# Four edits to a four-layer kernel: one scratch tile, the place of some clearings, an early bias, and the order of the last half block

## The chip, the cores and the metric

The kernel runs on one core of a Trainium2 chip. The core has five engines with their own instruction queues: TensorE (PE in the profile, its weight loads PEld), VectorE (DVE), ScalarE (ACT), GpSimd (POOL) and SyncE (SP), which here issues DMAs. They run side by side and wait for each other through semaphores. The metric is the device time of one execution in microseconds. Before the change it is 1390.49 us, the median of three runs (1388.63 to 1393.59).

## The reference, cut to what matters

Four transformer layers, each an attention and a feed-forward part, on 8 x 512 tokens of 128 columns in float32. Every part normalizes its input and adds its output to the residual:

```python
x = x + _L0_attn_ref(_layernorm(x), ...)   # spiking linear attention
x = x + _L0_ffn_ref(_layernorm(x), ...)    # 16 experts, top 2, gelu
x = x + _L1_attn_ref(_layernorm(x), ...)   # linear attention, elu + 1
x = x + _L1_ffn_ref(_layernorm(x), ...)    # gated, with chosen rows through 8 experts
x = x + _L2_attn_ref(_layernorm(x), ...)   # softmax attention, 16 heads of 64
x = x + _L2_ffn_ref(_layernorm(x), ...)    # low-rank experts, top 2, gelu
x = x + _L3_attn_ref(_layernorm(x), ...)   # causal convolution of 21 taps
x = x + _L3_ffn_ref(_layernorm(x), ...)    # fp4 quantized silu(gate) * up, then down
```

In the last part both the input and `h = silu(gate) * up` are rounded to a 4-bit grid in blocks of 16: the block's largest magnitude over 6 is the scale, the quotients are rounded, and the result is multiplied by the scale again. In layer 2's attention the queries have a bias `q_b`, and the scores are divided by 8.

## The kernel before, in words

The tokens lie in eight blocks of 512, each held on chip as 128 partitions by 4 tiles by 128 columns (`x[b]`). The program is recorded in the order in which the code is written; each engine executes its own instructions in that order, and waits where an operand comes from another engine. Tiles come from pools. A pool's tag has a number of buffers that are handed out in turn, and when a pool is closed, the next one's tiles take its memory: the first instruction that writes there waits for the last ones that used the old tiles.

*Layer 0's feed-forward part* (`layer0`) runs 128 units, one for each block and expert. For each unit TensorE makes the hidden values, ScalarE the Gelu, TensorE the second product, VectorE multiplies by the gate into a tile `pr` (line 607, in `second_half`), and GpSimd adds `pr` to the block's sum (line 611). `pr` comes from the pool `f0`, which is closed after the layer.

*Layer 1* (`layer1`) first records some preparations: two columns of ones in the tiles `vts`, a row of ones in the three tiles `zts` (line 1274), a matrix `top_row` with a first row of ones (lines 1275 and 1276), two small loads `ebs`, a tile `nought` of zeros (line 1281), and 15 DMAs from SP that write `nought` to device memory (seven to `back`, line 1283, eight to `slots_in`, line 1288). Then a loop over eight iterations runs the list `stages`; a stage with lag k works on block i + k. Among them are `project_q` (TensorE, then on ScalarE a Relu, line 880, and an exponential, line 881), `project_kv`, the key map (VectorE, line 885), `gather` (keys by values on TensorE), `attend`, `finish` (layer 0's last product for the blocks 3 to 7), and norms: mean and variance on VectorE (lines 758 to 761), reciprocal root on GpSimd (lines 246 and 247), scaling on ScalarE (line 769). `f_scale` stores each block's normalized rows by SP to `by_rows`, from where GpSimd gathers the chosen rows after the loop (line 1066). After the loop comes a hand-written order for the chosen rows; its last instructions scatter rows to `back` (line 1233) and add to the residual on GpSimd (line 1052 and line 1378).

*Layers 2 and 3* (`late`) run in 64 frames, one for each block and pair of heads, with the steps of layer 2's experts and layer 3 hung into them. The first instruction scales the query bias on VectorE (`qb`, line 2652, with the weights' blob `a2` as input); `queries` then makes keys on VectorE (line 1560) and queries on ScalarE (line 1559, which reads `qb`), and `first_scores` multiplies them.

*The end* (`end`) works off the last two blocks of layer 3: L is block 6, and A and B are the halves of block 7 (two tiles each). For each of them `quant_x1` and `quant_x2` round the input, `turn_x` transposes it, `gated` makes gate and up products and a tanh on ScalarE, and `gated_v` the factors. With `at_end` and `thirds`, ScalarE also copies half of up to a tile `prod` (line 2161), VectorE makes `(tanh + 1) * gate` (line 2164), and GpSimd multiplies the two (line 2166); without `thirds` VectorE does the second product too (line 2168). `quant_h1` (`fp4_scale`, lines 1401 to 1406) finds the blocks' scales and quotients. `fp4_round` rounds (VectorE: mask, line 1418; scaling of the mask, line 1421; add and subtract, lines 1422 and 1423) and multiplies by the scale on GpSimd (line 1424). `turn_h` transposes (line 2216) and copies (line 2219), `down` makes the last product, adds it to the residual (line 2100) and stores the rows (line 2239). `keep_clock(n)` issues n matmuls of 128x128 whose results nobody reads. The order is that of the code:

```python
                L.down()
                keep_clock(6)
                B.turn_x()
                ...
                B.quant_h1(1)
                A.turn_h(0)
                B.quant_h2_tile(1, 0)
                B.quant_h2_tile(1, 1)
                A.down()
                keep_clock(22)
                B.turn_h(1)
                B.down()
```

Of the kernel before, what the change touches and what calls it, by code (L numbers as in the profile page):

```python
# [17 lines left out]
F32 = mybir.dt.float32  # L18
# [146 lines left out]
def body(ctx, tc, dram, spans, x_in, ib, it, ic, ei, out):  # L165
# [114 lines left out]
    acc = []  # L280
    last_acc = first.tile([P, NB - 3, TB], F32, tag="acc", name="acc")
# [5 lines left out]
    def layer0():  # L287
# [7 lines left out]
        with ExitStack() as st:  # L295
# [302 lines left out]
            def second_half(b, e, hm, gs):  # L598
                po = bank()
                for i in range(4):  # L600
                    mm(
                        po[32 * i : 32 * (i + 1), :],
                        w2[:, e, :, :].rearrange("p a o -> p (a o)"),
                        hm[:, i, :],
                    )
                pr = acc[b] if e == 0 else wp.tile([P, TB], F32, tag="pr", name="pr")
                nc.vector.scalar_tensor_tensor(  # L607
                    pr, po, f0["b2"][:, e : e + 1], gs, ALU.add, ALU.mult
                )
                if e > 0:  # L610
                    nc.gpsimd.tensor_tensor(acc[b], acc[b], pr, ALU.add)  # L611
# [245 lines left out]
    def layer1():  # L857
# [9 lines left out]
        with tc.tile_pool(name="l1", bufs=2) as wp, tc.tile_pool(name="l1c", bufs=1) as once:  # L867
# [398 lines left out]
            with tc.manual_schedule():  # L1266
# [6 lines left out]
                for zt in zts:  # L1273
                    nc.gpsimd.memset(zt[64:65, :], 1.0)
                nc.gpsimd.memset(top_row, 0.0)
                nc.gpsimd.memset(top_row[:1, :], 1.0)
# [3 lines left out]
                nought = wp.tile([P, J, D], F32, tag="zo", name="nought")  # L1280
                nc.gpsimd.memset(nought, 0.0)
                for b in range(1, NB):
                    nc.sync.dma_start(
                        back[b * TB : (b + 1) * TB, :].rearrange("(j p) d -> p j d", p=P), nought
                    )
                for b in range(2):
                    blank[b] = [
                        nc.sync.dma_start(
                            slots_in[b][k * TB : (k + 1) * TB, :].rearrange("(j p) d -> p j d", p=P),
                            nought,  # L1290
                        ).ins
                        for k in range(4)
                    ]
                for i in range(NB):
                    for f, lag in stages:
                        if 0 <= i + lag < NB and (f, i) != (turn_, 0):
                            f(i + lag)
# [135 lines left out]
    def late():  # L1433
# [11 lines left out]
        with tc.tile_pool(name="a2", bufs=2) as wp, tc.tile_pool(name="l3", bufs=1) as lp:  # L1445
            N = NB * 8
            qb = wp.tile([P, 8], F32, tag="qb", name="qb", bufs=1)
# [582 lines left out]
            def layer3(b, xp, tile_, part=(0, J), conv_bank="one", h_tag="h"):  # L2030
# [156 lines left out]
                def quant_h2_tile(i, j):  # L2187
                    sc, a = t["fh", i]
                    k = slice(22 * j, 22 * (j + 1))
                    h = tile_("h", h_tile)  # L2190
                    fp4_round(lp, h[:, 2 * i + j, :], sc[:, k], a[:, k, :], 22)
# [31 lines left out]
                def down():  # L2223
                    ht = tile_("ht", None)
                    po = bank()
                    for j in range(j0, j1):
                        for k, _ in thirds:
# [6 lines left out]
                            )  # L2234
                    added(po)
# [149 lines left out]
            def end():  # L2385
# [51 lines left out]
                L.down()  # L2437
                keep_clock(6)
                B.turn_x()
                B.gated(2, True)  # L2440
                B.gated(3, True)
# [209 lines left out]
            with tc.manual_schedule():  # L2651
                nc.vector.tensor_scalar(qb, a2["qb"], 0.125, None, ALU.mult)
# [93 lines left out]
```

## Time and profile before

| | us |
|---|---|
| median of three runs | 1390.49 |
| the profiled execution, its own time | 1387.75 |
| its span, first to last instruction | 1385.6 |
| PE busy | 1323.9 (96%) |
| DVE busy | 1024.1 (74%) |
| ACT busy | 1011.0 (73%) |
| POOL busy | 646.3 (47%) |
| mean granted TensorE clock | 0.997 of full speed |

The profile is of one execution, whose times count from its first instruction. A line of the timeline gives the start, the duration, the engine, the line of the kernel, the instruction, its output and inputs by the program's names, the shape, and how many instructions of one kind are merged; in brackets stand the idle time of that engine just before, and what ended it. Line numbers in the text are those of the kernel before.

Layer 0 ends and layer 1 begins at about 381 us of the span, layer 1 ends at about 499 us, and the end part begins at about 1326 us.

### The profile page before, as it was taken

To read this page: it belongs to the slowest core of one execution; us is meant where nothing else is said; L and a number is where in the kernel's file an instruction comes from. 1 tells how busy PE (TensorE), PEld (TensorE's weight loads), DVE (VectorE), ACT (ScalarE), POOL (GpSimd) and SP (SyncE) were. 2 spreads that over 40 slices of the span, in tenths; PEclk is the share of its full clock that TensorE was granted. 3 is DMA by queue.
4 is the path that set the end of the run, shared out by engine and by line. 5 is a ranking of instruction groups with operands and counts; after the bars stand their busy time and mean duration, and the time that the engine had idled before them with its cause. 6 is when DMAs were issued, how large, how long until landed. Compare 5 with 4: busy or idle time off the path is not lost.

```text
span 1385.6 us, 33142 instructions
## 1 busy us (share of the span) xinstructions
PE 1323.9 (96%) x12910; PEld 704.4 (51%) x12910; DVE 1024.1 (74%) x2173; ACT 1011.0 (73%) x2050; POOL 646.3 (47%) x758
## 2 busy tenths in 40 slices
PE   7889999999989899999999999999999999999997
PEld 3762222222277655547447455555555555555576
DVE  6786666677477778863783689788788897887876
ACT  6859999999977656655684686777767767667632
POOL 6756667765632533230472453453443634424432
PEclk9999999999999999999999999999999999999999
DMA  5015555555280111241201101102011010110000
GB/s 181 1 25 163 170 145 149 150 152 145 62 278 28 28 40 35 65 115 30 73 21 36 45 2 22 31 2 43 11 23 23 9 33 20 23 23 10 2 9 16
DMA packets 125309, 84.47 MB, mean 61 GB/s; under 512 B 61984, under 2 KB 103712, under 8 KB 124769
## 3 DMA queue, kind: packets, MB, share of 16 engines
q1 hardware_dynamic: 123423, 78.43, 20.3%
q0 software_dynamic: 1152, 2.36, 0.6%
q8 instruction: 102, 1.67, 0.5%
q10 hardware_dynamic: 578, 1.57, 0.3%
q14 instruction: 54, 0.44, 0.1%
HBM read 64.29 MB, written 22.23 MB: 62 GB/s over the span
## 4 chain that ended last, share of the span: by engine, by line
PE 37%; DVE 14%; ACT 10%; issue 2%; POOL 1%; DMA 0%; DVEq 0%; ACTq 0%; POOLq 0%
PE ps L250 27%; PE ps L1598 8%; ACT ex L1677 6%; DVE nm L1671 5%; ACT prod L2065 2%; DVE acc L2051 1%; PE ps L2248 1%; DVE fa L1422 1%; DVE fa L1406 1%; ACT q L1559 1%; DVE fsc L1401 1%; ACT xn L1481 1%; DVE fa L1423 1%; DVE fm L1418 1%; DVE k L1560 1%
## 5 line engine op out<-in xcount | busy, mean ns | idle before, releaser
L1677 ACT ACTIVATE ex<-ps,nm 128x512 f32<-128x512 f32 x512 | 345.2, 687 | 172.3 <-DVE nm L1671 172.2
L1671 DVE TENSOR_REDUCE nm<-ps 128x2 f32<-128x1024 f32 x256 | 300.9, 1210 | 39.1 <-PE ps L250 39.0
L250 PE MATMUL ps<-q,k 64*64 64x512 f32 (+1 forms) x2240 | 258.3, 564 | 8.9 <-ACT ex L1677 5.7
L250 PE MATMUL ps<-ex,vs 128*64 128x512 f32 x1024 | 233.8, 598 | 1.1 <-DVE sm L1691 1.1
L1692 POOL TENSOR_TENSOR vs<-v,sm 128x256 f32<-128x256 f32 x128 | 78.6, 614 | 292.9 <-DVE sm L1691 268.6
L1598 PE MATMUL ps<-xt,blob_a 64*64 64x512 f32 x912 | 207.8, 589 | 0.1
L611 POOL TENSOR_TENSOR acc<-acc,pr 128x512 f32<-128x512 f32 x120 | 165.9, 1382 | 87.2 <-DVE pr L607 78.8
L595 ACT ACTIVATE hm<-ps,blob_f 128x1536 f32<-128x1536 f32 x128 | 196.2, 1533 | 0.0
L607 DVE SCALAR_TENSOR_TENSOR pr<-ps,blob_f,gs 128x512 f32<-128x512 f32 x120 | 90.0, 750 | 87.2 <-PE ps L250 76.6
L250 PEld LDWEIGHTS ps<-q,k 64*64 64x64 f32 x2240 | 74.8, 132 | 152.0 <-ACT ex L1677 78.2
L250 PE MATMUL ps<-h,w 32*128 32x512 f32 x1024 | 148.3, 643 | 1.1 <-ACT hm L594 0.6
L250 PEld LDWEIGHTS ps<-ex,vs 128*64 128x64 f32 x1024 | 68.0, 136 | 152.9 <-issue 128.1
L250 PE MATMUL ps<-hm,w 128*32 128x512 f32 x1024 | 136.8, 606 | 5.1 <-DVE pr L607 2.7
L2066 POOL TENSOR_TENSOR acs<-acs,prod 128x512 f32<-128x512 f32 x96 | 124.0, 1292 | 23.9 <-ACT prod L2065 19.4
L1598 PE MATMUL ps<-blob_a,ct 64*64 64x128 f32 x1824 | 118.6, 269 | 0.0
L1598 PE MATMUL ps<-blob_a,xt 64*64 64x128 f32 x1824 | 118.5, 269 | 0.0
L1598 PEld LDWEIGHTS ps<-blob_a,ct 64*64 64x64 f32 x1824 | 106.2, 133 | 0.0
L1677 ACT ACTIVATION_READ_ACCUMULATOR ex<-ps,nm 128x1 f32 x512 | 105.0, 205 | 0.0
L1598 PEld LDWEIGHTS ps<-blob_a,xt 64*64 64x64 f32 x1824 | 103.0, 133 | 0.0
L250 PEld LDWEIGHTS ps<-h,w 32*128 32x128 f32 x1024 | 41.1, 183 | 108.7 <-ACT hm L594 103.4
L594 ACT ACTIVATE hm<-ps,blob_f 128x512 f32<-128x512 f32 x128 | 88.0, 687 | 8.5 <-PE ps L250 8.3
L1598 PEld LDWEIGHTS ps<-xt,blob_a 64*64 64x64 f32 x912 | 61.7, 133 | 31.9 <-issue 28.4
(366 smaller groups left out, 2212.3 us busy)
## 6 DMA issues: line engine op xcount, KB each, us to landing
gs<-gates SPq DMA_DIRECT2D x248, 128.0 KB, 3.0
gates<-plain SPq DMA_DIRECT2D x16, 256.0 KB, 3.2
ht<-turned_h SPq DMA_DIRECT2D x20, 180.0 KB, 2.8
turned_h<-hb SPq DMA_DIRECT2D x40, 88.0 KB, 2.3
blob_f<-in_f SPq DMA_DIRECT2D x1, 2560.0 KB, 9.2
blob_a<-in_a SPq DMA_DIRECT2D x1, 2056.0 KB
x<-in_x SPq DMA_DIRECT2D x8, 256.0 KB, 5.7
plain<-turned SPq DMA_DIRECT2D x32, 64.0 KB, 2.2
```

The lines of the kernel that those rows point to most:

```text
L250: nc.tensor.matmul(out_, lhs, rhs, start=start, stop=stop)
L594: nc.scalar.activation(hm[:, 0, :], p1, AF.Gelu, bias=bias)
L595: nc.scalar.activation(hm[:, 1:, :], p3, AF.Gelu, bias=bias)
L607: nc.vector.scalar_tensor_tensor(pr, po, f0["b2"][:, e : e + 1], gs, ALU.add, ALU.mult)
L611: nc.gpsimd.tensor_tensor(acc[b], acc[b], pr, ALU.add)
L1401: nc.vector.tensor_reduce(sc, s3, AX.X, ALU.max, apply_absolute_value=True)
L1598: ins = nc.tensor.matmul(*args, **kw).ins
L1671: nc.vector.tensor_reduce(nm, ps, AX.X, ALU.max, negate=True)
L1677: nc.scalar.activation(ex[kt][:, i, :], ps[:, i, :], AF.Exp, bias=nm[:, i : i + 1], accum_out=sm[:, kt, i : i + 1],)
L1692: nc.gpsimd.tensor_tensor(vs[:, tiles, :, :], vs_[n][:, tiles, :].rearrange("p j (i n) -> p j i n", i=2), sm[:, tiles, :].unsqueeze(3).to_ ...
L2065: nc.scalar.activation(p, src, AF.Copy, scale=w)
L2066: nc.gpsimd.tensor_tensor(t["acs"], t["acs"], p, ALU.add)
```

## The change

1. In `second_half` the product of the very last unit (block 7, expert 15) is written to a tile of the pool `norm` (tag `xt`), which stays open through the whole kernel, and not to one of `f0`.
2. The fills of `zts`, `top_row` and `nought`, and the 15 DMAs that write zeros, are recorded at the start of the third iteration of layer 1's loop, not ahead of the loop. `vts` and `ebs` stay.
3. `qb` lies in the pool `const`, and is scaled at the start of the fifth iteration of layer 1's loop.
4. In `end`, `gated` of the tiles 2 and 3 (half B) is called without `thirds`. `down` is split into products and output: L's products move behind B's `gated`, into another PSUM bank, and L's residual add and store behind `A.down()`. B's last rounding is done by a new `quant_h2_pair`: mask and its scaling for both tiles at once, add and subtract tile by tile, and the last product for the first tile on GpSimd and for the second on VectorE. The calls of `keep_clock` become 17 and 13, where they were 6, 8 and 22.

```diff
+                elif (b, e) == (NB - 1, 15):
+                    pr = norm.tile([P, TB], F32, tag="xt", name="pr")
...
                 for i in range(NB):
+                    if i == 2:
+                        cleared()
+                    if i == 4:
+                        nc.vector.tensor_scalar(qb, a2["qb"], 0.125, None, ALU.mult)
                     for f, lag in stages:
...
+                def quant_h2_pair(i):
                     sc, a = t["fh", i]
+                    m = lp.tile([P, 44, 16], F32, tag="fm44", name="fm")
+                    nc.vector.tensor_scalar(
+                        m.bitcast(I32), a.bitcast(I32), 0x7F800000, None, ALU.bitwise_and
+                    )
+                    nc.vector.tensor_scalar(m, m, 1.0, 1.5 * 2.0**22, ALU.max, ALU.mult)
+                    for j, engine in enumerate((nc.gpsimd, nc.vector)):
+                        k = slice(22 * j, 22 * (j + 1))
+                        nc.vector.tensor_tensor(a[:, k, :], a[:, k, :], m[:, k, :], ALU.add)
+                        nc.vector.tensor_tensor(a[:, k, :], a[:, k, :], m[:, k, :], ALU.subtract)
+                        engine.tensor_tensor(
+                            tile_("h", h_tile)[:, 2 * i + j, :].rearrange("p (n k) -> p n k", k=16),
+                            a[:, k, :],
+                            sc[:, k].unsqueeze(2).to_broadcast([P, 22, 16]),
+                            ALU.mult,
+                        )
...
                 B.quant_x2()
-                L.down()
-                keep_clock(6)
+                keep_clock(17)
                 B.turn_x()
-                B.gated(2, True)
-                B.gated(3, True)
+                B.gated(2, True, False)
+                B.gated(3, True, False)
                 A.quant_h1(0)
                 A.quant_h2(0)
                 B.gated_v(2)
                 B.gated_v(3)
-                keep_clock(8)
+                po = L.down_products(bank("c"))
                 B.quant_h1(1)
                 A.turn_h(0)
-                B.quant_h2_tile(1, 0)
-                B.quant_h2_tile(1, 1)
+                B.quant_h2_pair(1)
                 A.down()
-                keep_clock(22)
+                L.down_out(po)
+                keep_clock(13)
                 B.turn_h(1)
                 B.down()
...
             with tc.manual_schedule():
-                nc.vector.tensor_scalar(qb, a2["qb"], 0.125, None, ALU.mult)
                 xts[0] = t[0]["next"]
```

More of the change, by code (lines that the diff above doesn't have):

```diff
@@ L280, in body @@
     acc = []
+    qb = const.tile([P, 8], F32, tag="qb", name="qb")
     last_acc = first.tile([P, NB - 3, TB], F32, tag="acc", name="acc")
@@ L605, in second_half @@
                     )
-                pr = acc[b] if e == 0 else wp.tile([P, TB], F32, tag="pr", name="pr")
+                if e == 0:
+                    pr = acc[b]
+                elif (b, e) == (NB - 1, 15):
+                    pr = norm.tile([P, TB], F32, tag="xt", name="pr")
+                else:
+                    pr = wp.tile([P, TB], F32, tag="pr", name="pr")
                 nc.vector.scalar_tensor_tensor(
@@ L1272, in layer1 @@
                     nc.gpsimd.memset(v[:, :, P : P + 1], 1.0)
[L1273 to L1276, printed above, removed]
                 for k, name in enumerate(("eb1", "eb2")):
@@ L1279, in layer1, with cleared @@
                     nc.sync.dma_start(ebs[:, k, :], dram["rows"][:, lo:hi].partition_broadcast(P))
[L1280 to L1287, printed above, removed]
-                        nc.sync.dma_start(
[L1289 to L1293, printed above, removed]
+                def cleared():
+                    for zt in zts:
+                        nc.gpsimd.memset(zt[64:65, :], 1.0)
+                    nc.gpsimd.memset(top_row, 0.0)
+                    nc.gpsimd.memset(top_row[:1, :], 1.0)
+                    nought = wp.tile([P, J, D], F32, tag="zo", name="nought")
+                    nc.gpsimd.memset(nought, 0.0)
+                    for b in range(1, NB):
+                        nc.sync.dma_start(
+                            back[b * TB : (b + 1) * TB, :].rearrange("(j p) d -> p j d", p=P), nought
+                        )
+                    for b in range(2):
+                        blank[b] = [
+                            nc.sync.dma_start(
+                                slots_in[b][k * TB : (k + 1) * TB, :].rearrange("(j p) d -> p j d", p=P),
+                                nought,
+                            ).ins
+                            for k in range(4)
+                        ]
                 for i in range(NB):
+                    if i == 2:
+                        cleared()
+                    if i == 4:
+                        nc.vector.tensor_scalar(qb, a2["qb"], 0.125, None, ALU.mult)
                     for f, lag in stages:
@@ L1446, in late @@
             N = NB * 8
-            qb = wp.tile([P, 8], F32, tag="qb", name="qb", bufs=1)
             xts, vs_, qks, exs, outs, cts = {}, {}, {}, {}, {}, {}
@@ L2185, in quant_h2 @@
                     fp4_round(lp, pair(i), *t["fh", i], 44)
-                def quant_h2_tile(i, j):
+                def quant_h2_pair(i):
                     sc, a = t["fh", i]
-                    k = slice(22 * j, 22 * (j + 1))
-                    h = tile_("h", h_tile)
-                    fp4_round(lp, h[:, 2 * i + j, :], sc[:, k], a[:, k, :], 22)
+                    m = lp.tile([P, 44, 16], F32, tag="fm44", name="fm")
[12 more added lines that the diff above has]
+                            ALU.mult,
+                        )
                 def blocks_h(i):
@@ L2223, in down, with down_products @@
                 def down():
+                    down_out(down_products(bank()))
+                def down_products(po):
                     ht = tile_("ht", None)
-                    po = bank()
                     for j in range(j0, j1):
@@ L2234, in down, with down_out @@
                             )
+                    return po
+                def down_out(po):
                     added(po)
```

## The prediction

> **What bounds the kernel now.** The page first: one core, TensorE busy 96% at full clock, and a chain of waits that it can follow back only to 496 us.
>
> ```profile
> span 1385.6 us, 33142 instructions
> PE 37%; DVE 14%; ACT 10%; issue 2%; POOL 1%; DMA 0%; DVEq 0%; ACTq 0%; POOLq 0%
> ```
>
> So a share says little: the edits touch three short places, each with its own last wait. I read each in the timeline (start, duration, engine, line, and in brackets the idle time before it with its releaser). Place one is the hand-over from layer 0 to layer 1:
>
> ```profile
> 380.69 1.89 PE L250 MATMUL ps<-blob_l,xt 128*128 128x256 f32 x8
> 380.83 1.27 POOL L611 TENSOR_TENSOR acc<-acc,pr 128x512 f32<-128x512 f32 x1 [0.80 <-DVE pr L607]
> 382.13 0.60 ACT L880 ACTIVATE ex<-ps 128x512 f32<-128x512 f32 x1 [2.16 <-POOL acc L611]
> 383.29 0.58 ACT L880 ACTIVATE ex<-ps 128x512 f32<-128x512 f32 x1
> 384.86 0.23 POOL L246 TENSOR_SCALAR rs<-mv 128x4 f32<-128x4 f32 x1
> 386.53 1.65 ACT L769 ACTIVATE xn<-x,nb,rs 128x128 f32<-128x128 f32 x4 [1.03 <-POOL nb L763]
> ```
>
> ScalarE stands 2.16 us until GpSimd has added layer 0's last product. Place two is the start of layer 2:
>
> ```profile
> 498.38 1.28 POOL L1378 TENSOR_TENSOR x<-x,blob_bc 128x512 f32<-128x512 f32 x1
> 498.98 0.72 DVE L2652 TENSOR_SCALAR qb<-blob_a 128x8 f32<-128x8 f32 x1 [1.02 <-POOL x L1052]
> 499.61 0.74 DVE L1560 TENSOR_SCALAR k<-ps,blob_a 128x512 f32<-128x512 f32 x1
> 499.78 0.69 ACT L1559 ACTIVATE q<-ps,qb 128x512 f32<-128x512 f32 x1 [3.69 <-DVE qb L2652]
> 500.52 1.95 PE L250 MATMUL ps<-q,k 64*64 64x512 f32 x16 [1.86 <-ACT q L1559]
> ```
>
> An 8-column scaling stands ahead of the first keys and queries, and TensorE waits for both. Place three is the end, VectorE and GpSimd taking turns:
>
> ```profile
> 1362.72 0.69 DVE L2100 TENSOR_TENSOR x<-x,ps 128x512 f32<-128x512 f32 x1
> 1368.94 1.38 POOL L1424 TENSOR_TENSOR h<-fa,fsc 128x704 f32<-128x704 f32 x1 [4.07 <-DVE fa L1423]
> 1370.28 1.81 POOL L2166 TENSOR_TENSOR h<-s,prod 128x352 f32<-128x352 f32 x2
> 1372.12 0.89 DVE L1401 TENSOR_REDUCE fsc<-h 128x44 f32<-128x704 f32 x1 [2.47 <-POOL h L2166]
> 1376.90 0.81 DVE L1421 TENSOR_SCALAR fm<-fm 128x352 f32<-128x352 f32 x1
> 1378.91 0.79 POOL L1424 TENSOR_TENSOR h<-fa,fsc 128x352 f32<-128x352 f32 x1 [1.40 <-DVE fa L1423]
> 1382.03 0.42 DVE L2100 TENSOR_TENSOR x<-x,ps 128x256 f32<-128x256 f32 x1 [2.87 <-PE ps L250]
> ```
>
> VectorE idles 2.47 us for two GpSimd products queued behind a third; after the last quantization only transposes, copies and products remain.
>
> **The change, part by part.**
>
> *Last product in the norms' pool.* Layer 1's first Relu takes over layer 0's scratch memory, so it waits for the last reader of the `pr` buffers: the add that ends at 382.10. Now that reader is the add before (ended 380.02), and what ends last is the query projection on TensorE, ended 380.85. So the first Relu could start 1.25 us sooner. But the key Relu (383.29) reads a projection that TensorE ends at 380.69 + 1.89 = 382.58, so from there only 383.29 - 382.62 = 0.67 us is left. From the key Relu run, without slack, the exponential, the value copy, the key map (385.04) and TensorE's gather (385.83). I take 0.67; ends 0 and 1.25.
>
> *Clearings at the third iteration.* Out of GpSimd's queue go six fills, 382.35 to 384.78. They stood ahead of the reciprocal root at 384.86; ScalarE's 1.03 us idle goes, but its next Relu then waits for TensorE, so nothing is added to the 0.67. They come back where GpSimd idles 5.91 us (390.4 to 396.3): 2.4 us fit. Of the 15 zero-fill DMAs on SP the last was issued at 406.26, and the first store of normalized rows at 407.23. They now start about 7 us later but behind the same two weight loads (2,560 and 2,056 KB), which are what held them (one issue took 8.7 us). If that store slips, its reader is GpSimd's row gather at 462.42, over 50 us later. I count nothing; if both covers failed, the 2.4 us of fills would show.
>
> *Query bias early.* It comes to VectorE behind the fourth key map, at 409.3. Small scalings without company cost 0.17 to 0.18 us (line 1107, 128x18: 0.176); in this iteration VectorE takes up the gather's result without idling, so I charge 0.1, ends 0 and 0.72 (its row at 498.98). At the start of layer 2 the keys move up to 498.98, when VectorE's list of waits is done, and end at 499.72; ScalarE's queries no longer wait for `qb`, only for the same GpSimd add (ended 498.45) and scatter, and run beside the keys. TensorE starts at 499.78 instead of 500.52: 0.74. The old row ran to 499.70, when GpSimd's add at 498.38 ended. Would that add hold the keys too, the gain would be 0.1 at most. But all 64 key rows lie between 0.732 and 0.752 us, with GpSimd busy beside many, so I keep 0.74; ends 0 and 0.74.
>
> *The end.* (i) The residual add at 1362.72 moves behind the quantizations; the next reduction moves up by 0.61 (1362.72 to 1363.33), and all to the last rounding with it. (ii) The two GpSimd products (1.81) and two ScalarE copies are replaced by two VectorE instructions of 0.52. Four such instructions to the next reduction took 2.15 us at 1331.26 to 1333.41; so the reduction starts at 1368.71 - 0.61 + 2.15 = 1370.25, not 1372.12: 1.87 so far. GpSimd's 1.38 us product, which it must also await, ends at 1369.7. (iii) From that reduction to the mask took 2.53 us, unchanged. Mask and scaling run whole (1.12, from 1365.85 to 1366.97) and not twice by halves; then four half adds and subtracts and VectorE's own last product: 0.56 + 0.46 + 0.56 + 0.56 + 0.53 = 2.67. Ready at 1370.25 + 6.32 = 1376.57, where the old one was at 1379.70. (iv) GpSimd's half product (0.79) now runs amid VectorE instructions with two SBUF operands. These rows show what that costs:
>
> ```profile
> 112.11 1.28 POOL L611 TENSOR_TENSOR acc<-acc,pr 128x512 f32<-128x512 f32 x1
> 112.66 1.28 DVE L477 TENSOR_TENSOR one<-eq,place 128x512 f32<-128x512 f32 x1
> 731.48 1.29 POOL L2066 TENSOR_TENSOR acs<-acs,prod 128x512 f32<-128x512 f32 x1
> 732.71 0.63 POOL L1692 TENSOR_TENSOR vs<-v,sm 128x256 f32<-128x256 f32 x1
> 732.80 1.08 DVE L2097 TENSOR_TENSOR acc<-acc,acs 128x512 f32<-128x512 f32 x1 [0.43 <-POOL acs L2066]
> ```
>
> Alone this form takes 0.68 (median of line 462). Begun while GpSimd had 0.73 and 0.54 us to go, it lost 0.60 and 0.40: it stood until about 0.13 before GpSimd's end. Here GpSimd must first outlast one VectorE add, then holds back the next for its 0.79 less 0.13 at its end and, I estimate, 0.17 that pass before VectorE asks: about 0.49. Ready at 1377.06. [...] (v) The last tile's transposes wait for the residual add behind it (0.34 + 0.12): 1377.52, before 1379.75. From there the old end took 2.28 us, six products among them; three of these now run earlier, so 1.95. VectorE's last add starts at 1379.47, not 1382.03: 2.56. The moved products and the other filler matmuls lie on TensorE while it would idle: 12 products (2.94) end by 1370, when the transposes want it; 13 fillers of 0.23 end about 1375.5, before the first half is ready at 1376.3. Ends: 3.05 without the lock; 0.9 if the lock takes 1.5 (two of line 462's worst case, 1.43 - 0.68) and (i) gives nothing.
>
> Sum: 0.67 - 0.1 + 0.74 + 2.56 = 3.9 us. The profiled execution took 1387.75 with a span of 1385.6; it becomes 1383.9. It is below all three runs shown (median 1390.49), from which I take the same 3.9: 1386.6.
>
> **The rivals.**
> [...]
> - *The early gains are absorbed*, some later wait of layer 1 or 2 ending where it did: only the end counts, 2.5, 1388.0. For it: 100 us lie between place one and two. Against: each iteration of layer 1 is one ring, VectorE's kv at 403.18 to TensorE, back to VectorE at 407.13, to the key map at 408.63 and TensorE's gather, about 8.1 us a turn, and no landing is in it.
> - *The end is given back*: the moved 256 KB store now goes out about 1.5 us before the last, whose landing is the end. Stores of that size land in 2.3 us, of the last one's in 1.8; fully in line it loses about 1: 1387.6.
> - *Slower*: the early bias stands before VectorE's whole queue until its weight load lands. The zero-fill that waits for that load issued at 398.73, so it had landed 10 us before the bias; each microsecond past 409.3 would cost one, and from 413.2 on the kernel is slower. Landing at 415 gives 1392.3.
>
> **How the numbers follow.** Main case 0.46, lock free 0.21, absorbed 0.16, end given back 0.11, slower 0.06. The terms' bounds together give savings from 0.2 to 5.0 us, 1385.5 to 1390.3. The three runs lie 5 us apart, so a median moves by some 1.5; with that, 8 in 10 lie in 1383.8 to 1389.7. The bound of 0.3%, about what a measurement can tell from no change, is 4.2 us: 1386.3. The main case lies 0.3 above it, half of it falls on either side (0.24); of the lock-free 0.16, of the others 0.07 to 0.09: faster 0.48. Slower 0.06, and 0.46 within the bound.
>
> **What would show it.** First Relu near 381.0 and key Relu near 382.65; no idle before the layer's first norm scaling; fills in GpSimd's old gap. `qb` of 0.2 us near 409, TensorE's first scores directly behind the keys, some 1.3 us sooner. At the end a VectorE two-operand instruction of about 1.0 instead of 0.53 beside GpSimd's product, and 2.5 us from the last GpSimd wait gone. I am wrong if the first scores move by less than 1 us, or if the stretch from 1326 to the end shrinks by less than 2.

## The result and the profile after

The changed kernel takes 1387.13 us, the median of 14 runs (1385.73 to 1389.35); the kernel before, in as many runs beside it, 1391.41 us. The ratio is 0.9973, with a 95% interval of 0.9962 to 0.9985: 3.8 us of 1391.41, between 2.1 and 5.3; the two medians as such lie 4.3 us apart. Forecast were 3.9 us and 1386.6 us. The interval also holds 2.5 us, the end alone, and 4.4 us, the sum without the 0.49 for which VectorE was to stand beside GpSimd's product, so only the stages in the traces can tell these apart.

The profiled execution of the changed kernel is a surprise, though. It took 1389.20 us, which is more than the 1387.75 of the profiled execution before. First the page, its span and its chain of waits by engine:

```profile
span 1387.4 us, 33118 instructions
...
PE 38%; DVE 14%; ACT 10%; issue 2%; POOL 0%; DMA 0%; DVEq 0%; ACTq 0%; POOLq 0%; SPq 0%
```

These lines tell as little as before; what happened stands in the timeline of the three places. The hand-over from layer 0 to layer 1 (start, duration, engine, line, instruction, and in brackets the idle time and its releaser):

```profile
381.29 1.89 PE L250 MATMUL ps<-blob_l,xt 128*128 128x256 f32 x8
...
381.36 1.28 POOL L617 TENSOR_TENSOR acc<-acc,pr 128x512 f32<-128x512 f32 x1 [0.74 <-DVE pr L613]
381.61 0.60 ACT L886 ACTIVATE ex<-ps 128x512 f32<-128x512 f32 x1 [1.03 <-PE ps L250]
...
382.80 0.23 POOL L246 TENSOR_SCALAR rs<-mv 128x4 f32<-128x4 f32 x1
...
383.21 0.60 ACT L886 ACTIVATE ex<-ps 128x512 f32<-128x512 f32 x1 [0.34 <-PE ps L250]
...
385.77 1.13 PE L250 MATMUL ps<-v,k 128*128 128x129 f32 x8 [1.27 <-issue]
```

The first Relu (L886) waits for TensorE and no longer for GpSimd, which ends its add only at 382.64. The key Relu at 383.21 comes 0.03 us after the end of its projection (381.29 + 1.89 = 383.18). From the start of that projection to the first product of values and keys it takes 385.77 - 381.29 = 4.48 us; before it took 385.83 - 380.69 = 5.14, by this row of the kernel before:

```profile
385.83 1.13 PE L250 MATMUL ps<-v,k 128*128 128x129 f32 x8 [1.93 <-POOL rs L246]
```

Gained: 0.66.

The bias and the start of layer 2:

```profile
409.18 0.16 DVE L1307 TENSOR_SCALAR qb<-blob_a 128x8 f32<-128x8 f32 x1
...
498.52 1.28 POOL L1058 TENSOR_TENSOR x<-x,zo 128x512 f32<-128x512 f32 x1
499.75 1.27 POOL L1391 TENSOR_TENSOR x<-x,blob_bc 128x512 f32<-128x512 f32 x1
...
500.28 0.69 ACT L1571 ACTIVATE q<-ps,qb 128x512 f32<-128x512 f32 x1 [2.84 <-PE ps L250]
500.36 0.75 DVE L1572 TENSOR_SCALAR k<-ps,blob_a 128x512 f32<-128x512 f32 x1 [1.06 <-PE ps L250]
...
501.21 1.95 PE L250 MATMUL ps<-q,k 64*64 64x512 f32 x16 [1.20 <-DVE k L1572]
```

Keys and queries run side by side, and TensorE's scores start 501.21 - 498.52 = 2.69 us after the start of GpSimd's residual add; before it was 500.52 - 497.16 = 3.36, from this row:

```profile
497.16 1.29 POOL L1052 TENSOR_TENSOR x<-x,zo 128x512 f32<-128x512 f32 x1
```

Gained: 0.67. GpSimd's second add (499.75 to 501.02) lies over all but the last 0.09 us of the keys, and they took their usual 0.75.

The end:

```profile
1371.99 1.39 POOL L1437 TENSOR_TENSOR h<-fa,fsc 128x704 f32<-128x704 f32 x1 [4.06 <-DVE fa L1436]
...
1373.91 0.89 DVE L1414 TENSOR_REDUCE fsc<-h 128x44 f32<-128x704 f32 x1
...
1378.57 0.52 DVE L2208 TENSOR_TENSOR fa<-fa,fm 128x352 f32<-128x352 f32 x1
1378.80 0.93 POOL L2210 TENSOR_TENSOR h<-fa,fsc 128x352 f32<-128x352 f32 x1 [3.26 <-DVE fa L2209]
1379.12 0.99 DVE L2209 TENSOR_TENSOR fa<-fa,fm 128x352 f32<-128x352 f32 x1
...
1380.22 0.53 DVE L2210 TENSOR_TENSOR h<-fa,fsc 128x352 f32<-128x352 f32 x1
1380.37 0.48 ACT L2243 COPY ht<-ps 120x384 f32<-120x384 f32 x1 [5.44 <-PE ps L2240]
1380.66 1.01 DVE L2112 TENSOR_TENSOR x<-x,ps 128x256 f32<-128x256 f32 x2
...
1381.13 0.54 PE L2240 MATMUL ps<-blob_c,h 128*120 128x128 f32 x3 [0.80 <-DVE x L2112]
...
1381.50 2.26 PE L250 MATMUL ps<-wd,ht 120*128 120x128 f32 x12
...
1383.80 0.42 DVE L2112 TENSOR_TENSOR x<-x,ps 128x256 f32<-128x256 f32 x1 [2.13 <-PE ps L250]
```

I measure from the quotients of the last half's input on VectorE, which began at 1359.76 before and at 1363.53 now:

```profile
1359.76 0.42 DVE L1406 TENSOR_TENSOR fa<-xn,frc 128x256 f32<-128x256 f32 x1
...
1363.53 0.42 DVE L1419 TENSOR_TENSOR fa<-xn,frc 128x256 f32<-128x256 f32 x1
```

The reduction of the last half follows VectorE's own products without idle time, and h is ready at 1380.75, after 17.22 us; before it was ready after 1379.70 - 1359.76 = 19.94. That is 2.72 us. The subtract beside GpSimd's product takes 0.99, where the one of the first tile, without GpSimd beside it, takes 0.53. The last residual add, however, starts after 20.27 us, against 22.27: of 2.72 only 2.00 arrive. The last twelve products took 2.26 us because TensorE had half its clock from 1382.4 on (granted 0.50 from there to 1383.76; at full clock, in the run of the fourth edit alone below, they take 1.67).

Half-clock stretches are also where the profiled execution lost time that the edits have nothing to do with. This view shows windows of 2 us each near 467 us in the changed kernel (busy time by engine, then the granted clock, the share of the DMA engines and GB/s):

```profile
core 0: us, PE busy (x) PEld busy (x) DVE busy (x) ACT busy (x) POOL busy (x), PEclk, DMA share, GB/s
464.00:466.00 2.00, 1.42 (x12) 1.07 (x10) 1.47 (x10) 0.00 (x0) 1.89 (x3) 1.00 0.22 66
466.00:468.00 2.00, 1.21 (x7) 1.00 (x7) 0.00 (x0) 0.37 (x1) 1.76 (x5) 0.91 0.00 0
468.00:470.00 2.00, 2.00 (x4) 0.99 (x4) 1.27 (x9) 0.19 (x1) 0.10 (x1) 0.50 0.00 0
470.00:472.00 2.00, 2.00 (x5) 0.94 (x4) 1.07 (x7) 0.39 (x1) 0.00 (x0) 0.74 0.00 0
```

From 467.6 to 471.0 TensorE ran at half clock (0.50), right where the chosen rows' products wait for it; before's profile has a granted clock of 1.00 there. The span adds up as follows (after less before, between marks that both traces have):

| stretch | after less before, us |
|---|---|
| start to layer 1's key projection | +0.60 |
| key projection to the first product of values and keys | -0.66 |
| from there to the last residual add of layer 1 (half clock near 467) | +1.43 |
| that add to layer 2's first scores | -0.67 |
| first scores to the last half's quotients (layers 2 and 3; half clock near 799) | +3.07 |
| quotients to the last residual add | -2.00 |
| last residual add to the end | +0.05 |
| sum | +1.82 |

The three stretches that the edits touch shrank, as forecast. The others were longer in this one execution.

### The profile page after: what moved, and what is told of

Its sections match the earlier page's. It is cut to its first block, busy times and chain, and to the rows that moved or that the text cites. A ratio compares the mean times of both kernels' runs of the same rounds, so it can differ in the third digit from the quotient of the medians.

```text
span 1387.4 us, 33118 instructions
## 1 busy us (share of the span) xinstructions
PE 1326.6 (96%) x12898; PEld 705.1 (51%) x12898; DVE 1024.4 (74%) x2174; ACT 1011.3 (73%) x2048; POOL 644.5 (46%) x755
## 3 DMA queue, kind: packets, MB, share of 16 engines
q8 instruction: 102, 1.67, 0.5%
## 4 chain that ended last, share of the span: by engine, by line
PE 38%; DVE 14%; ACT 10%; issue 2%; POOL 0%; DMA 0%; DVEq 0%; ACTq 0%; POOLq 0%; SPq 0%
PE ps L250 28%; PE ps L1610 8%; ACT ex L1689 5%; DVE nm L1683 4%; ACT prod L2077 2%; DVE acc L2063 1%; PE ps L2277 1%; DVE fa L1419 1%; DVE fa L1435 1%; DVE fsc L1414 1%; ACT q L1571 1%; ACT xn L1493 1%; DVE k L1572 1%; DVE fa L1436 1%; DVE s L2176 1%
```

## The experiments

**The first two edits apart.** The kernel before with only the scratch tile of the last unit changed:

```diff
-                pr = acc[b] if e == 0 else wp.tile([P, TB], F32, tag="pr", name="pr")
+                if e == 0:
+                    pr = acc[b]
+                elif (b, e) == (NB - 1, 15):
+                    pr = norm.tile([P, TB], F32, tag="xt", name="pr")
+                else:
+                    pr = wp.tile([P, TB], F32, tag="pr", name="pr")
```

> The kernel before with the first edit alone (layer 0's last product in the norms' pool; the clearings stay ahead of the loop). Theory: the reused scratch tile alone held layer 1 back. The first Relu no longer stands 2.16 us for GpSimd, the key Relu starts within 0.05 us of the end of its projection, and TensorE's first product of values and keys comes 4.48 us after the start of the key projection, as in the changed kernel, not 5.14 as before. The fills still delay the first norm's scaling on ScalarE, but nothing waits for that: the 0.67 us are still there at 410 us and when layer 2 starts. Ratio 0.9995. Rival, the clearings must go too: the product comes after 4.48 us, but the next blocks are as late as before, nothing is left at 410 us, ratio 1.0000.

Its timeline at the hand-over:

```profile
379.27 1.89 PE L250 MATMUL ps<-blob_l,xt 128*128 128x256 f32 x8
...
381.20 0.60 ACT L885 ACTIVATE ex<-ps 128x512 f32<-128x512 f32 x1 [0.34 <-PE ps L250]
...
383.27 0.23 POOL L246 TENSOR_SCALAR rs<-mv 128x4 f32<-128x4 f32 x1
...
383.76 1.13 PE L250 MATMUL ps<-v,k 128*128 128x129 f32 x8 [1.27 <-POOL rs L246]
...
384.93 1.26 ACT L774 ACTIVATE xn<-x,nb,rs 128x128 f32<-128x128 f32 x3 [1.51 <-POOL nb L768]
```

4.49 us from projection to product, and that with all fills in place: GpSimd's reciprocal root starts 4.00 us after the projection (1.51 in the changed kernel), ScalarE idles 1.51 us for it, and the product comes at the same moment all the same. The third small VectorE copy of the loop (`kc`) still comes 0.64 us sooner after the projection than before (21.21 against 21.85), and so does the eighth, at 446 us in the kernel before. Ratio 0.9992 (0.9978 to 1.0006). The clearings are not needed for the gain.

The second edit alone, the other half of the pair:

```diff
                 for i in range(NB):
+                    if i == 2:
+                        cleared()
```

> The kernel before with the second edit alone (the clearings at the third iteration). Theory: nothing; the first Relu still waits for GpSimd's last add, the product of values and keys comes 5.1 us after the start of the key projection, and the fills lie in GpSimd's old gap. Ratio 1.0000, change below 0.1 us from there to the start of layer 2. Rival, the fills held the loop: up to 0.67 us sooner at 410 us, ratio 0.9995.

5.15 us from projection to product, and ratio 0.9997 (0.9982 to 1.0011). Its profile has half-clock windows at 384.4 and 469.7; from the first on everything is 1.6 us later, at 394 us (1.56) as at 446 us (1.58). What the fills took in their new place lies under the first of these half-clock windows and can't be read here. The changed kernel shows it: its third and eighth `kc` come 21.19 and 64.99 us after the projection, against 21.21 and 65.01 with the first edit alone, so the fills cost nothing there. GpSimd's reciprocal root does come early (1.70 us after the projection), and it helps nothing.

**The third edit alone.**

```diff
+    qb = const.tile([P, 8], F32, tag="qb", name="qb")
...
                 for i in range(NB):
+                    if i == 4:
+                        nc.vector.tensor_scalar(qb, a2["qb"], 0.125, None, ALU.mult)
...
-                nc.vector.tensor_scalar(qb, a2["qb"], 0.125, None, ALU.mult)
```

> The kernel before with the third edit alone (the query bias scaled in layer 1's fifth iteration). Theory: the scaling costs VectorE 0.16 us where it had slack; at the start of layer 2 the first scores come 2.69 us after the start of GpSimd's residual add, not 3.36: 0.67 us gained, nothing lost at 410 us, ratio 0.9995. Rival, absorbed: the scores come sooner but the first stages of layer 2 take it back, so that nothing is left at 600 us, ratio 1.0000.

```profile
501.26 1.28 POOL L1053 TENSOR_TENSOR x<-x,zo 128x512 f32<-128x512 f32 x1
...
503.94 1.52 PE L250 MATMUL ps<-q,k 64*64 64x512 f32 x12 [1.19 <-DVE k L1562]
```

2.68 us from GpSimd's add to the scores. In the loop, the time from one `kc` to the next over the inserted scaling is 8.09 us, as in the kernel before (410.63 - 402.54): the 0.16 us cost nothing. The 33rd row maximum of layer 2 on VectorE starts 88.1 us after the first scores, in this kernel as in the one before, so nothing is taken back by then. Ratio 0.9977 (0.9961 to 0.9993), 3.2 us; 0.9995 lies just outside. By the trace the edit is worth 0.67 us, and I have no mechanism for more; five of its twelve runs had a mean clock of 0.999 or 1.0, of the first two edits' 23 runs two.

**The fourth edit alone.** The diff is the whole of the end's part of the change (`quant_h2_pair`, `down_products`, `down_out` and the new order).

> The kernel before with the fourth edit alone (the order of the last half block). Measured from the quotients of the last half's input on VectorE (1359.76 before) the last product of h is ready after 19.94 us in the kernel before and after 17.22 in the changed one; the last residual add starts after 22.27 and 20.27. Theory: this edit is most of the gain, 2.7 us at h and as much at the last residual add when TensorE runs its last products at full clock (19.55 to 19.7); in the changed kernel's profile a half-clock window at the end took 0.6 to 0.75 of it. Ratio 0.9980 to 0.9985. Rival, the window belongs to the new order (more idle TensorE ahead of the last products): it is there again, 20.3 us and 2.0 us, ratio 0.9986 to 0.999. Rival, half of the gain is from the first three edits (1.3 of 3.8 by their stages): then the sum of the single ratios falls short of the whole's 0.9973.

```profile
1381.37 1.67 PE L250 MATMUL ps<-wd,ht 120*128 120x128 f32 x12
...
1383.07 0.42 DVE L2100 TENSOR_TENSOR x<-x,ps 128x256 f32<-128x256 f32 x1 [1.54 <-PE ps L250]
```

h is ready after 17.22 us and the last add starts after 19.69, at full clock: 2.58 us less than before. The new order does not bring the half clock by itself, and the 2.00 of the changed kernel's profile was an accident of that execution. Ratio 0.9989 (0.9975 to 1.0004), below what the trace says but within its reach. The single ratios together give 0.8 + 0.3 + 2.3 + 1.1 = 4.5 thousandths, each with some 1.5 to either side, against 2.7 for the whole: the runs are too few for a sum. The stages give 0.66 + 0.67 + 2.58 = 3.9 us.

**What GpSimd's product costs VectorE.** The changed kernel with both last products on VectorE:

```diff
-                    for j, engine in enumerate((nc.gpsimd, nc.vector)):
+                    for j, engine in enumerate((nc.vector, nc.vector)):
```

> The changed kernel with both last products of h on VectorE, so that GpSimd does nothing beside them. All times from the quotients of the last half's input on VectorE, as in the run of the end alone (h ready after 17.22, last residual add after 19.69 at full clock; the second subtract took 0.99). Theory, GpSimd's product holds VectorE's subtract: that takes 0.53 now, VectorE has a product of 0.56 more in its row and 0.46 less of waiting, h is ready after 17.3 and the last add starts after 19.7 to 19.8: no change. Rival, the subtract is slow by itself (its place, its operands): still 0.99, h after 17.78, last add after 20.2.

```profile
1379.93 0.52 DVE L2209 TENSOR_TENSOR fa<-fa,fm 128x352 f32<-128x352 f32 x1
```

0.52 instead of 0.99: the subtract is not slow by itself. h is ready after 17.32 us, 0.10 later, and the last add starts after 19.53, 0.16 sooner, since the last transposes now wait for VectorE's product only (why no longer for the residual add, no run shows). One run took 1388.71 us. The product on GpSimd thus buys nothing; VectorE loses 0.46 of the 0.56 that it saves.

A second test with the product left on GpSimd, and the first half's residual add put in the place where VectorE stands:

```diff
                         nc.vector.tensor_tensor(a[:, k, :], a[:, k, :], m[:, k, :], ALU.add)
+                        if j == 1:
+                            between()
                         nc.vector.tensor_tensor(a[:, k, :], a[:, k, :], m[:, k, :], ALU.subtract)
...
-                B.quant_h2_pair(1)
-                A.down()
+                pa = A.down_products(bank())
+                B.quant_h2_pair(1, lambda: A.added(pa))
+                A.stored()
```

> The changed kernel with the first half's residual add (one operand from SBUF, one from PSUM) put between VectorE's second add and second subtract, in the time that the subtract stood. Theory, only VectorE instructions with two SBUF operands are held: the residual add takes 0.42 beside GpSimd's product, the subtract behind it 0.55 to 0.6, h is ready after 17.27 instead of 17.22, and the last tile's transposes no longer wait 0.33 for the residual add: last add after 19.4 instead of 19.69. Rival, any VectorE instruction that touches SBUF is held: the residual add takes about 0.9, the subtract 0.53, h after 17.7, last add after 19.8. Times from the quotients of the last half's input, at full clock.

```profile
1377.46 0.93 POOL L2212 TENSOR_TENSOR h<-fa,fsc 128x352 f32<-128x352 f32 x1 [3.27 <-DVE fa L2211]
1377.66 0.41 DVE L2112 TENSOR_TENSOR x<-x,ps 128x256 f32<-128x256 f32 x1
1377.99 0.78 DVE L2211 TENSOR_TENSOR fa<-fa,fm 128x352 f32<-128x352 f32 x1
```

The residual add, with one operand in PSUM, takes its 0.41 in the middle of GpSimd's product. The subtract behind it, with two operands in SBUF, takes 0.78, until 0.38 us after GpSimd's end at 1378.39: it resumed about 0.15 before that end (1377.99 + 0.78, less the 0.53 that it takes alone). (I had expected 0.55 to 0.6; the subtract was issued 0.33 us after the residual add and not after its whole 0.41, so it stood longer.) That only instructions with two operands in SBUF stand is not shown: the kernel before has a scaling of the mask, with one operand there, that took 0.81 at 1376.90 while GpSimd's product ran until 1377.51, and 0.34 at 1375.03. h is ready after 17.23, the last add starts after 19.44, 0.26 sooner than with the change. Ratio 0.9976 (0.9964 to 0.9988), not to be told from the change by the clock.

**The wait of the last transposes.**

```diff
-                A.down()
+                A.down_out(A.down_products(bank("o")))
```

> The changed kernel with the first half's last products in another PSUM bank, so that the last tile's transposes take a bank that was read long before and need not wait for the residual add. Theory: h as before after 17.22, transposes 0.05 us behind it and not 0.38, last add after 19.36 instead of 19.69 at full clock. Rival, ScalarE's first copy or the products of the tile ahead set the end: transposes sooner, last add still after 19.6 to 19.7.

The last transposes start 0.15 us behind h, no longer 0.38, and the last add after 19.43 us: 0.26 gained of the 0.33 that I expected, since TensorE takes 0.15 to start on VectorE's product. Ratio 0.9975 (0.9964 to 0.9987).

**Where the end is still bound.** From the last half's input to h VectorE of the changed kernel is busy for 16.32 of the 17.22 us and waits for nothing that the trace shows, so I kept the other bank and took work from VectorE where GpSimd has nothing to do:

```diff
-    def fp4_round(pool, dst, sc, a, blocks, room=None):
+    def fp4_round(pool, dst, sc, a, blocks, room=None, last=None):
...
-        nc.vector.tensor_tensor(a, a, m, ALU.subtract)
+        (last or nc.vector).tensor_tensor(a, a, m, ALU.subtract)
...
-                A.quant_h2(0)
+                A.quant_h2(0, nc.gpsimd)
...
-                keep_clock(13)
+                keep_clock(10)
```

> The same with two things more: the subtract of the first half's rounding goes from VectorE to GpSimd, which idles there, and 10 filler matmuls instead of 13. Theory: VectorE is the row that sets the end, and the four products behind the subtract read PSUM and one tile of SBUF, so GpSimd holds none of them: GpSimd's subtract takes 1.4 us, VectorE's row is shorter by 0.93, h ready after 16.3, last add after 18.4 to 18.5 at full clock; against the changed kernel 1.2 us, ratio to the kernel before about 0.9964. Rival, GpSimd's subtract holds VectorE's products too: h after 17.0 to 17.2, nothing gained but the bank's 0.33. Rival, the first half is late then (GpSimd has two instructions of 1.4 us in a row) and its transposes, copies and products come between: h after 16.3, last add after 19.

```profile
1367.74 1.68 POOL L1436 TENSOR_TENSOR fa<-fa,fm 128x704 f32<-128x704 f32 x1 [3.08 <-DVE fa L1435]
...
1369.51 1.39 POOL L1437 TENSOR_TENSOR h<-fa,fsc 128x704 f32<-128x704 f32 x1
1370.92 0.89 DVE L1414 TENSOR_REDUCE fsc<-h 128x44 f32<-128x704 f32 x1 [1.29 <-POOL h L1437]
```

It missed: h after 17.48, last add after 19.69, ratio 0.9980 (0.9968 to 0.9992). VectorE's four products were not held (0.51 to 0.52 each), but the reduction behind them stood 1.29 us for GpSimd's product. It writes the tile of the blocks' scales (`fsc`), of which there is one, and GpSimd's product still read the first half's. And GpSimd's subtract of two full operands takes 1.68, not 1.4.

With a second buffer for that tile:

```diff
-        sc = pool.tile([P, room], F32, tag=f"fsc{room}", name="fsc", bufs=bufs)[:, :blocks]
+        sc = pool.tile([P, room], F32, tag=f"fsc{room}", name="fsc", bufs=2 if room == 44 else bufs)[:, :blocks]
```

> The version with the first half's subtract on GpSimd, and two buffers for the tile of the blocks' scales, whose single buffer made the last half's reduction wait 1.29 us for GpSimd's product. Theory: the reduction follows VectorE's products directly, h is ready after 16.2 to 16.45 (the small scaling behind the reduction may stand for GpSimd's product for up to 0.25), the last add starts after 18.4 to 18.65 at full clock, 1.0 to 1.3 sooner than in the changed kernel. Rival, another buffer takes the place of that one (the quotients are written over those that GpSimd still reads): h after 17.0 or later.

```profile
1369.89 1.39 POOL L1437 TENSOR_TENSOR h<-fa,fsc 128x704 f32<-128x704 f32 x1
1370.05 0.89 DVE L1414 TENSOR_REDUCE fsc<-h 128x44 f32<-128x704 f32 x1
1370.97 0.35 DVE L1416 TENSOR_SCALAR frc<-fsc 128x44 f32<-128x44 f32 x1
```

The reduction overlaps GpSimd's product unharmed; the small scaling behind it takes 0.35 instead of 0.19 until that product ends at 1371.28. h after 16.46, last add after 18.66: 1.03 us sooner than with the change, 0.26 of it from the bank. Median 1386.02 us, ratio 0.9969 (0.9959 to 0.9980).

Then the last rounding without GpSimd, over both tiles at once:

```diff
-                    for j, engine in enumerate((nc.gpsimd, nc.vector)):
+                    nc.vector.tensor_tensor(a, a, m, ALU.add)
+                    nc.vector.tensor_tensor(a, a, m, ALU.subtract)
+                    for j in range(2):
                         k = slice(22 * j, 22 * (j + 1))
-                        nc.vector.tensor_tensor(a[:, k, :], a[:, k, :], m[:, k, :], ALU.add)
-                        nc.vector.tensor_tensor(a[:, k, :], a[:, k, :], m[:, k, :], ALU.subtract)
-                        engine.tensor_tensor(
+                        nc.vector.tensor_tensor(
```

> The same, and the last rounding without GpSimd: add and subtract over both tiles at once (0.89 each), then the two last products on VectorE (0.56 each). Theory: 2.95 us instead of 3.17 from the scaling of the mask to h, since nothing is held and one instruction of 704 columns is cheaper than two of 352; h after 16.0 to 16.2, last add after 18.2 to 18.4. Rival, the two tiles now come within 0.56 us of each other and their transposes, copies and products queue up: last add no sooner than with GpSimd's product.

The rival was right: h 0.29 sooner (16.17), but the last add after 18.61, only 0.05 sooner. The two tiles' copies on ScalarE now follow each other (0.91 us for two) and the twelve products start together behind them. Ratio 0.9975 (0.9965 to 0.9985), median 1386.82.

**Half-clock windows.** The changed kernel again, on the same chip as the last two:

> The changed kernel once more, beside the versions built on it. Theory: the three stages are as in its profile (4.48, 2.69 and 17.22 us at their marks; 19.69 at the last add unless a half-clock window lies over it), and what differs between runs is how many half-clock windows fall beside gaps of TensorE (near 467 and 799 us), about 1.5 us each, and layers 2 and 3 by up to 4 us. Ratio 0.9973 as before. Rival: the whole's ratio is nearer to 1 because the layers 2 and 3 got longer by the change: stretch from the first scores to the last half's quotients 862 again, not 859 to 860.

4.49, 2.69 and 17.23 us at the three marks and 19.70 at the last add: the stages repeat to 0.01 us. Ratio 0.9975 (0.9963 to 0.9987). Half clock fell from 465.3 to 472.1 and at 799.8, and the stretch of layers 2 and 3 took 863.5 us. This kernel does not refute the rival. The single edits speak against it: 862.4 with the first alone, 863.3 with the second, 861.6 with the third, 862.5 with the fourth, though none of them touches layers 2 and 3 between those marks. If the second edit itself made that stretch 4.1 us longer than the 859.2 of the kernel before, its ratio would be near 1.003, outside its interval (0.9982 to 1.0011); so the one profile of the kernel before is more likely a short case. A second profile of that kernel would settle it.

Last, fillers in the gap near 465 us, on top of the version with whole rounding:

```diff
                 for m in range(2):
                     nc.tensor.transpose(cols(ps, m), c_["row", m], ident)
+                    for _ in range(3 - m):
+                        mm(cols(ps, 3), ident, ident)
```

> The same, and five filler matmuls beside the two transposes of the gathered rows in layer 1, where TensorE idles near 465 us and most profiles so far have a half-clock window at 464 to 470 us. Theory: the window is due to that gap and no longer falls there; the stretch from the first product of values and keys to the residual add is 111.3 us as in the kernel before's profile, not 112.8 to 114.8, and the median falls by about 1 us against the same kernel without the fillers. Rival, five short matmuls do not fill enough: a window falls there as often as before.

Median 1383.00 us (1382.34 to 1383.32, 5 runs), ratio 0.9948 (0.9935 to 0.9962): faster than both kernels, and its interval lies just apart from that of the changed kernel beside it. Its profile has no half clock before the end, and 111.56 us in the stretch that took 111.33 before. Near 465 us the fillers did change something: this profile and the last one of the changed kernel both got full clock for the first time 14.75 us after their first instruction, and layer 1's key projection starts at 378.78 and 378.98. In the first profile of the changed kernel every half-clock window starts a whole multiple of 3.413 us behind the first full clock (20, 26, 132, 229 and 400 times), and the 465.3 of the second one fits 132. Counted so, stretches of 3.41 us lie alike over both, within 0.2 us; for the profile with fillers, which has no window there, that is an estimate. From 461.9 to 465.3 TensorE was busy for 1.62 us without fillers, and half clock followed; with them it was busy for 2.70, and none followed. That is one pair of profiles. Whether the five matmuls made the median is open: 1 us was expected, 3.8 came. The profile of the version without them has no half clock there either (110.82 us), though all five runs with fillers have a mean clock of 0.999 or 1.0. The profile with fillers also lacks the windows near 85 and 105 us, which come ahead of the fillers, and the one near 799. The one run without fillers at clock 1.0 took 1381.81 us. Five runs that agree in this may share another cause.

## Why the prediction was right

- *Last product in the norms' pool: 0.67, measured 0.66.* The choice that mattered was to count from the key Relu and the end of its projection, not from the first Relu's 2.16 us wait. The first Relu now starts 0.32 us after the projection's start, 1.44 before; of these 1.12 us only 0.66 reach the product.
- *Clearings: nothing, measured nothing*, and shown from both sides: the first edit alone has the whole gain with the fills in the way, the second alone has none up to the first product. The fills lie at 390.40 to 392.84, the zero fills are issued from 392.86 to 406.03, and the first store of normalized rows at 406.16 did not slip.
- *Query bias early: 0.1 charged, measured 0.00.* The instruction takes 0.16, in slack.
- *Start of layer 2: 0.74, measured 0.67.* The keys start 1.84 us after GpSimd's add began, as reckoned (1.82). Of the 0.07, 0.04 are TensorE's start behind VectorE: scores begin 0.10 after the keys' end, where I had put 0.06; the rest is 0.02 of a later start and 0.01 of the keys' length. GpSimd's add over the keys did not hold them; the doubt priced at 0.1 was settled in favour of the 64 key rows.
- *The end: 2.56, measured 2.58 (2.00 in the profile that half clock disturbed).* Step by step: (i) and (ii) 1.87 to the reduction, measured 1.98; (iii) 2.53 to the mask again 2.53; mask, scaling and halves with (iv) 1.12 + 2.67 + 0.49 = 4.28, measured 4.31; the held subtract 0.49, measured 0.46; (v) 2.41 from h to the last add, measured 2.47 in the run of the fourth edit alone. So the end's 0.02 is partly luck: (i) gave 0.72 and not 0.61, and 0.03 and 0.06 behind it took most of that back. The 0.46 has luck in it too: GpSimd's product took 0.93 and not 0.79, and 0.32 of it and not 0.17 had passed before VectorE asked. The fillers end at 1379.11, before the first transposes at 1379.79.
- *The sum: 3.9, measured 3.9 by stages and 3.8 by runs.* Here too errors nearly cancel: the 0.10 charged for the bias was not paid, and the start of layer 2 gave 0.07 less. The absolute 1386.6 was 0.5 low, since the kernel before has a median of 1391.41 over 14 runs and had 1390.49 over three.
- *The signs of being wrong.* In the two profiles as they stand both appear: the first scores come 0.69 us later (501.21 against 500.52) and not 1 us sooner, and the stretch from ScalarE's last copy ahead of the end part (1326.89 before, 1330.65 now) to the end shrank by 1.94 us, just less than 2. Half clock did that, and for the scores also the 0.60 us ahead of the key projection. The two profiles with all four edits and no half clock near 467, those of the whole rounding without and with fillers, have the first scores 117.99 and 118.72 us after the key projection, against 119.83 before; and the fourth edit alone shortens the end by 2.58. The signs should have been given between marks.

*Lock free* (0.21): the lock stands in the forecast for the 0.49 us that VectorE loses beside GpSimd's product. That it costs nothing is refuted by the two tests of it: 0.99 for the subtract with the product beside it against 0.52 without, and 0.78 in the second test, where an instruction with one operand in PSUM took 0.41. These rows of the kernel before would speak for it:

```profile
1346.79 1.02 POOL L247 TENSOR_TENSOR rs<-rs,half 128x2 f32<-128x2 f32 x1
1347.27 0.89 DVE L1422 TENSOR_TENSOR fa<-fa,fm 128x704 f32<-128x704 f32 x1
...
1356.46 0.72 POOL L247 TENSOR_TENSOR rs<-rs,half 128x2 f32<-128x2 f32 x1
```

VectorE's two-operand add kept its 0.89, and GpSimd's 128x2 product beside it took 1.02, where that form took 0.72 at 1356.46, so there GpSimd lost time; why there and not VectorE, no run shows. Moving the product to VectorE does not bring h sooner either, since it costs 0.56 there itself. Of the rivals, *absorbed* is refuted for the first edit up to 446 us and for the third up to 88 us into layer 2; further on the spread of layers 2 and 3 is larger than the gains. *The end is given back by the store*: from the last add to the end it takes 3.64 us, 3.59 before. *Slower through the early bias*: the scaling at 409.18 waited for nothing.

What failed is the sentence that the profiled execution "becomes 1383.9". It became 1389.20. The step took one execution as a base and the sum of the edits as the only difference; layers 2 and 3 alone differ by 4.4 us between the profiles here, of which the kernel before's is the shortest of all (859.2, others 860.9 to 863.7). The forecast of the median held since I took the 3.9 from the runs' median and not from that execution.

## What to carry to other kernels

When a wait goes, look for the next instruction that cannot move and price the edit there: 2.16 us of idle ScalarE were worth 0.66, and 2.4 us of fills ahead of a reciprocal root were worth nothing. An idle GpSimd next to a busy VectorE helped here under VectorE instructions that read PSUM (0.51 to 0.52 each) or reduce (0.89); under a two-operand SBUF subtract (0.99, alone 0.52) it took back nearly what it saved, 0.46 of 0.56, and a tile with one buffer undid the rest (1.29 us of waiting). With edits of under 0.1%, measure between marks in the trace, where 0.01 us repeats; the runs here could not tell 0.7 us from nothing.

## What I had not expected of the hardware

Half-clock windows of 3.41 us come and go with a kernel that does not change. They fell near 464 to 472 us in nine of the fourteen profiles, near 799 us (795 to 801) in six, and once over the last products. From layer 1's first product of values and keys to its last residual add the profiles without such a window took 110.8 to 111.6 us, those with one of 3.41 near 467 us 112.6 to 113.3, those with 6.83 us there 114.7 to 114.9. In the 3.40 us ahead of the changed kernel's windows near 467, 799 and 1382 us TensorE had been busy for 2.04, 1.30 and 1.92 us, so a window does not need a TensorE that is idle throughout; in the run of the end alone 1.93 us ahead of the last products brought none, so busy time alone does not decide it. The half-clock windows that the end of the run does not cut last 3.41 us or twice that, at a granted clock of 0.50. In the profiles whose starts I give they lie whole multiples of 3.413 us apart: in the changed kernel 20.48 us from the one near 85 to the one near 106 (6 times), 361.81 from there to the one near 467 (106) and 331.09 on to the one near 799 (97), in its second profile 334.5 (98), in the run of the second edit alone 85.3 (25). That the place of these starts against the kernel's own work differs from run to run, and that this is why the same kernel has the windows or not, is my guess from these numbers. The nine profiles whose first full clock came 15.8 to 17.5 us after the first instruction all have a window near 85 us; the five in which it came after 13.9 to 14.8 us have none. No run here shows a cause. Over 87 runs of the kernel before, a mean granted clock lower by 0.001 went with 1.0 us more, from 1387.63 us at 1.000 to 1399.27 at 0.991.

Open remains why layers 2 and 3 took from 859.2 to 863.7 us with the same instructions; a window near 799 us is about 1.2 us of it (from the 65th to the 97th row maximum 120.5 to 120.8 us with one, 118.7 to 119.5 without). One piece I could find: near 667 us of the changed kernel VectorE takes up a product of TensorE 1.2 us after its end (669.03 against 667.80), where before it did so after 0.1 (666.93 against 666.82). The trace has the update of the semaphore that VectorE waits for there only at 668.94 (666.83 before), so the delay lies on TensorE's side of the signal; its cause wasn't tried.
